# A two-layer graph attention network on one core: the carried row as column 0 of the one-hot matrix, nodes moved up by one

## The chip, the core and the metric

The kernel runs on one core of a Trainium2 chip. The core has five engines that run side by side, each with its own queue of instructions: TensorE (PE, matrix products into PSUM; PEld is its weight load), VectorE (DVE), ScalarE (ACT), GpSimd (POOL) and SyncE (SP, which here only issues DMAs). Data move between HBM and the on-chip memory through 16 DMA engines. The metric is the device time of one execution in microseconds (us); lower is better.

## The reference

There are 6,250 nodes with 256 features and 200,000 edges that are sorted by destination. After a layer norm and a ReLU come two graph attention layers (4 heads of 64, then 1 head of 256). In each, every edge has a logit, made of a value of its source, a value of its destination and a value of its 32 edge attributes; the logits go through a softmax over the edges of one destination; and the rows of the sources are summed with these weights at the destination. One loop edge per node, with the mean of the edge values, is added. Cut to what matters:

```python
te = relu(edge_attr @ We + be) * exp(x @ Wo + bo)[src][:, None]
s2, d2, ea2 = _add_self_loops(src, dst, te, n)
hx = (x @ Wg).reshape(n, h, f)
al = leaky_relu(a_s.hx[s2] + a_d.hx[d2] + a_e.(ea2 @ Wge), 0.2)
m = segment_max(al, d2)
al = exp(al - m[d2])
al = al / segment_sum(al, d2)[d2]
out = segment_sum(hx[s2] * al[:, :, None], d2) + b
```

## The kernel before

**Steps.** The sorted edges are cut into 66 steps of 24 x 128 = 3,072 edges (the last two are shorter). Both layers run through all steps, 132 in all. The edges of a step end at some 96 neighbouring nodes; `base` is the first of them. A node's place in a step is its number less `base`, and 128 places are provided for (partition = place).

**One step.** GpSimd gathers the source rows of the edges, 24 indirect DMAs of 128 rows each, into a tile G (three buffers), with a small memset between two gathers. TensorE makes the edge values from the attributes (`rphase1`, line 1014, and `rphase2`, line 1028) and spreads the destinations' values to the edges (`parts`, `adst`). VectorE adds the logits, runs maximum scans along the edges (`logits`, `links`, `maxima`; TensorE transposes in between, lines 1138 and 1155) and multiplies G by the weights (`scale`, line 1223). A one-hot matrix S (128 edges x 128 places, 24 of them; line 1058, VectorE) says which edge belongs to which place, and 24 accumulating products of S with G (`sums`, line 1234) sum the rows at the places. `evict` copies the sums from PSUM to U (line 1239, ScalarE). `finish` of the step before makes the output rows out of U.

**The carried row.** A node's edges can begin in one step and end in the next. So the sum of a step's last node is carried on: `carry` multiplies U by a one-hot column `lsel` (1 at the place of the last node) on TensorE (line 1245), which moves that row to partition 0, and copies it out of PSUM (line 1247, ScalarE). In the next step, after `scale`, `carried` adds this row, with a factor for the changed maximum, to edge 0 of partition 0 in G, ahead of `sums`.

**Order.** The order on each engine is written out by hand in `edges` (and `tight` and `last` for the last steps of a layer). In a full step k: GpSimd's gathers of step k+1; logits, transposes and maxima of k; edge values of k+1; scale, carried and sums of k; edge rows and one-hots of k+1; finish of k-1; evict and carry of k. Behind the carry on TensorE stand, in layer 0, the transposes of `turned` (line 1329), which write the same single PSUM buffer `fin`, and then the transpose of line 1138 of the next step.

**Loads and stores on SyncE.** `nodes` loads the node rows of a step, up to three steps ahead, into `tw` (five buffers): from table T, 268 columns in layer 0 (line 995), with x, 256 columns, beside it (line 997); 516 columns from the second table in layer 1. `load_ea` fetches edge attributes for two steps (one buffer, line 955), `load_lb` the places of the edges, which four groups of 32 partitions get as copies. `rows3` stores the rows of a finished step: 520 columns into the second table in layer 0 (line 1370), 256 into the output in layer 1 (line 1375; the last two steps by an indirect DMA). Neighbouring steps' rows overlap; the later store wins.

**Constants.** `kps` is a PSUM tile with the row 0..127 (`k_iota`), compared with each edge's place to give S, and its first 32 columns, compared for the smaller one-hot Q in `spread`. `qsel` and `lsel` are made in `indices`, which also counts whatever doesn't fit (more than 128 places and the like) into a flag; then a general path would compute everything again.

Of the kernel before, what the change touches and what calls it, by code (L numbers as in the profile page):

```python
# [22 lines left out]
F32 = mybir.dt.float32  # L23
# [8 lines left out]
P = 128  # L32
# [46 lines left out]
class Kernel:  # L79
# [31 lines left out]
    def consts(self, wp):  # L111
        nc, cp, a = self.nc, self.cp, self.a
        V = nc.vector
        self.ident = cp.tile([P, P], F32, name="ident")
        make_identity(nc, self.ident)
        self.wg, row, wpk = [], [], []
        self.ones = cp.tile([P, 1], F32, name="ones")
        nc.gpsimd.memset(self.ones, 1.0)
        self.bias, self.webd, self.be, wge = [], [], [], []
        for L in self.L:  # L120
            q = (nc.scalar, nc.sync)[L.l]
            wg = cp.tile([P, 2, L.MW], F32, name=f"wg{L.l}")
# [24 lines left out]
        self.kps = k = self.ps_k.tile([P, 512], F32, name="kps")  # L147
        V.tensor_copy(k[:, 0:P], self.iota_f)
        m32 = wp.tile([P, 1], F32, name="m32", bufs=1)
        self.quad = cp.tile([P, 4], F32, name="quad")  # L150
        nc.gpsimd.memset(self.quad, 0.0)
        for i in range(4):
            r = slice(32 * i, 32 * i + 32)
            nc.gpsimd.memset(m32[r, :], -32.0 * i)
            nc.gpsimd.memset(self.quad[r, i:i + 1], 1.0)
        V.tensor_add(k[:, P:P + 1], self.iota_p, m32)
        self.k_iota, self.k_part, self.k_w = k[:, 0:P], k[:, P:P + 1], k[:, 2 * P:2 * P + 4 * C + 4]
        self.wea = []
        for L in self.L:
            wea = cp.tile([P, PH], F32, name=f"wea{L.l}")  # L160
            nc.gpsimd.memset(wea, 0.0)
            self.wea.append((wea, cp.tile([P, L.H], F32, name=f"we1{L.l}")))

        def fold(L):

            H = L.H
            for k in range(2):
                for j, c0 in ((0, L.p), (1, L.ad)):
                    t = wp.tile([P, D], F32, name="wtmp", bufs=4)
                    V.tensor_mul(t, self.wg[L.l][:, k, 0:D], row[L.l][:, j, :])  # L170
                    yield
                    V.tensor_reduce(self.wg[L.l][:, k, c0:c0 + H], t.rearrange("p (h f) -> p h f", h=H),
                                    axis=AX.X, op=OP.add)
                    yield

        def fold_e(L):

            H = L.H
            wea, we1 = self.wea[L.l]
            t = wp.tile([P, D], F32, name="wtmp", bufs=4)  # L180
            V.tensor_mul(t, wge[L.l], row[L.l][:, 2, :])
# [12 lines left out]

        return fold(self.L[0]), later()
# [234 lines left out]
    def indices(self, wp):  # L430
# [26 lines left out]
        V.tensor_sub(qd, base.unsqueeze(1).to_broadcast([P, 4, NS]), qbase)  # L457
        yield
        self.qsel = cp.tile([P, NS, 4], F32, name="qsel")
        V.tensor_scalar(self.qsel.rearrange("p s k -> p k s"), qd, self.iota_p, None, op0=OP.add)  # L460
        yield

        bcf = wp.tile([NS, 4], F32, name="bcf", bufs=1)
# [31 lines left out]
        V.tensor_copy(self.base_i[:, 0, :], base[0:1, :])  # L495
        V.tensor_scalar(self.base_i[:, 1, :], base[0:1, :], float(N - P), None, op0=OP.min)
        yield
        ll = wp.tile([P, NS], F32, name="ll", bufs=1)
        V.tensor_sub(ll, last, base)
        self.lsel = cp.tile([P, NS], F32, name="lsel")  # L500
        V.tensor_scalar(self.lsel, ll, self.iota_p, None, op0=OP.is_equal)
        yield
        self.slink = cp.tile([1, NS], F32, name="slink")
        V.tensor_tensor(self.slink, sc0[0:1, 0, :], sc0[0:1, 2, :], op=OP.is_equal)
# [2 lines left out]

        chk = wp.tile([1, 9, NS + 1], F32, name="chk", bufs=1)
        V.memset(chk, 0.0)
        V.tensor_scalar(chk[:, 0, :NS], ll[0:1, :], float(P - 1), None, op0=OP.is_gt)  # L510
        V.tensor_sub(qd[0:1], qlast[0:1], qbase[0:1])
        V.tensor_scalar(chk[:, 5:9, :NS], qd[0:1], 31.0, None, op0=OP.is_gt)
        nb = wp.tile([1, NS + 1], F32, name="nb", bufs=1)
# [1 line left out]
        yield  # L515
        V.memset(nb[:, NS:], float(N))
        V.tensor_sub(nb[:, :NS], nb[:, 1:], nb[:, :NS])
        V.tensor_scalar(chk[:, 1, :NS], nb[:, :NS], float(P), None, op0=OP.is_gt)
# [92 lines left out]
    def edges(self, ctx):  # L611
# [11 lines left out]
        steps = self.steps  # L623
        self.state = {0: None, 1: None}
        self.early = 0
        self.nodes(steps[0])
        self.gather(steps[0], self.CX)
        if self.NS % 2:
# [15 lines left out]
        for k, st in enumerate(steps):  # L644
# [51 lines left out]
            if enter:  # L696
                pr = pv
            else:
                self.evict(st)
                self.carry(st)  # L700
                if pv:
                    self.rows1(pv)
                    late = pv
# [23 lines left out]
    def tight(self, st, pv, pr, nx):  # L727
# [36 lines left out]
            self.rows3(pv)  # L764
        drain(self.maxima(st))
        if final:
            self.carry(pv)
            drain(y)
            self.load_ea(st["k"] + 2)
        else:  # L770
# [1 line left out]
        self.rphase2(nx)  # L772
        self.adst(nx)
        if not final:
            self.carry(pv)
            if pr:
                self.rows1(pr)
                self.rows2(pr)
# [10 lines left out]
    def last(self, st, pv, nx):  # L789
# [20 lines left out]
        drain(self.maxima(st))  # L810
        if pv:
            self.evict(pv)
            self.carry(pv)
        drain(self.scale(st, 3))
        self.carried(st)
        self.sums(st)
# [172 lines left out]
    def nodes(self, st):  # L989
        nc, L, s = self.nc, st["L"], st["s"]  # L990
        r = self.row(0, s)
        tw = self.np_.tile([P, self.L[0].TW + D], F32, name="tw", bufs=5)
        st["tw"], st["xw"] = tw[:, :L.TW], tw[:, L.TW:L.TW + D]
        w = L.TW + L.l * D
        nc.sync.dma_start(tw[:, :w], self.T[L.l][ds(r, P), 0:w])
        if L.l == 0:
            nc.sync.dma_start(st["xw"], self.a["x"][ds(r, P), :])

    def halves(self, st):

# [30 lines left out]
    def spread(self, st):  # L1031
# [6 lines left out]
        if len(q) < 2 or q[0]["C"] != q[1]["C"]:  # L1038
# [3 lines left out]
        Q = self.wp.tile([P, 2, P], BF, name="Q")  # L1042
        V.tensor_tensor(lb[:, :, :n], lb[:, :, :n], self.k_part.unsqueeze(2).to_broadcast([P, i, n]), op=OP.is_equal)  # L1043
        V.tensor_tensor(Q[:, :i].rearrange("p i (k j) -> p (i k) j", j=32),
                        self.k_iota[:, 0:32].unsqueeze(1).to_broadcast([P, 4 * i, 32]),
                        self.qsel[:, s:s + i, :].rearrange("p i k -> p (i k)").unsqueeze(2)
                        .to_broadcast([P, 4 * i, 32]), op=OP.is_equal)
        for j, t in enumerate(q):
# [2 lines left out]
    def onehots(self, st, c0=0, c1=C):  # L1051
        nc, o = self.nc, st["o"]
        c1 = min(c1, st["C"])
        if "S" not in st:
            st["S"] = self.sp.tile([P, C, P], F32, name="S")
        if c0 < c1:
            w = [P, c1 - c0, P]
            nc.vector.tensor_tensor(st["S"][:, c0:c1, :], self.k_iota.unsqueeze(1).to_broadcast(w),  # L1058
# [138 lines left out]
    def carried(self, st):  # L1197


        if st["prev"] is not None:  # L1200
            L, V = st["L"], self.nc.vector
            H, pr = L.H, st["pr"]
            g, cv = st["G"][0:1, 0, :], st["prev"]["carry"]
            if H == 1:
                V.scalar_tensor_tensor(g[:, :D + 1], cv[0:1, :D + 1], pr[:, 0:1], g[:, :D + 1], op0=OP.mult, op1=OP.add)
            else:
# [29 lines left out]
    def evict(self, st):  # L1236
        L = st["L"]
        st["U"] = U = self.np_.tile([P, 272], F32, name="U", bufs=3)
        self.nc.scalar.activation(U[:, :L.W], st["u"][:, :L.W], AF.Copy)  # L1239

    def carry(self, st):
        nc, L, s, U = self.nc, st["L"], st["s"], st["U"]
        if s + 1 < self.NS:
            pr = self.ps_f.tile([P, 512], F32, name="fin")
            nc.tensor.matmul(pr[0:1, :L.W], self.lsel[:, s:s + 1], U[:, :L.W], start=True, stop=True)  # L1245
            st["carry"] = cv = self.wp.tile([1, 272], F32, name="carry")
            nc.scalar.activation(cv[:, :L.W], pr[0:1, :L.W], AF.Copy)

    def merge(self, st, wp, w):

# [114 lines left out]
    def rows3(self, st):  # L1365
        nc, L, s = self.nc, st["L"], st["s"]
        if L.l == 0:
            self.table_row(st)
            r = self.row(0, s)
            nc.sync.dma_start(self.T[1][ds(r, P), :], st["trow"])  # L1370
            return
        o, out = st["o"], self.a["out"]
        if s < self.direct:
            r = self.row(1, s)
            nc.sync.dma_start(out[ds(r, P), :], o)
        else:
            idx = self.np_.tile([P, 1], I32, name="oidx")
            nc.vector.tensor_add(idx, self.base_f[:, s:s + 1], self.iota_p)
            nc.gpsimd.indirect_dma_start(
                out=out[:, :], out_offset=bass.IndirectOffsetOnAxis(ap=idx[:, 0:1], axis=0), in_=o,  # L1380
                in_offset=None, bounds_check=self.N - 1, oob_is_err=False)
# [215 lines left out]
```

## Time and profile before

| | |
|---|---|
| device time, median of 3 runs | 4717.75 us (4715.25 to 4721.8) |
| the profiled execution, device time | 4718.23 us |
| its span on the core | 4716.0 us |
| TensorE busy (products) | 3214.2 us, 68% |
| VectorE busy | 2878.5 us, 61% |
| ScalarE busy | 574.2 us, 12% |
| GpSimd busy | 3701.8 us, 78% |
| gathers, GpSimd line 928 | 3102 issues, 0.959 us each |
| products u of `sums`, line 1234 | 6252 records, 393 ns each |
| carry: product, line 1245 | 260 records, 613 ns each |
| gather queue (q0) | 422.75 MB, 33.8% of the 16 DMA engines' span |
| SyncE's DMA queue (q1) | 158.16 MB, 10.1% |

The share of busy time says little by itself here: no engine is busy all the time, since a step is a chain over several engines. The prologue and the turn between the layers (about 2300 to 2530 us) apart, the span consists of equal steps, first of layer 0 and then of layer 1. The ends of TensorE's products in the trace are modelled: it records 24 products of `sums` in about 11 us, and the eviction that waits for the last of them begins some 19 us after the first.

```profile
PE   7777767777677776777655666666666666656666
DVE  7566767667676676766743555546455555645555
POOL 5688888888888888888648888888888888888884
DMA  6344444444444444444323444444444444444442
```

Each digit is the busy share, in tenths, in one of 40 equal slices of the span: one sees the two layers, and the turn in the middle.

### The profile page before, as it was taken

What the parts mean: (1) busy time and instruction counts of PE and PEld (TensorE: products, weight loads), DVE (VectorE), ACT (ScalarE), POOL (GpSimd) and SP (SyncE); (2) the same over time, 40 slices, a digit from 0 to 9 for tenths busy, and PEclk for the clock granted to TensorE, in tenths of its full rate; (3) what the DMA queues carried; (4) which work ended last, traced back from release to release, by engine and by line L of the source; (5) the groups of instructions that cost most, each with busy time, mean ns of one, the idle gap of its engine ahead of it and who ended that gap; (6) DMA issues with size and microseconds to landing.
All of it is one profiled execution on the core that took longest, in us unless ns stands there. A gap on an engine that the chain in (4) does not pass through costs nothing.

```text
span 4716.0 us, 38255 instructions
## 1 busy us (share of the span) xinstructions
PE 3214.2 (68%) x10176; PEld 1915.8 (41%) x10176; DVE 2878.5 (61%) x6552; ACT 574.2 (12%) x1282; POOL 3701.8 (78%) x6350
## 2 busy tenths in 40 slices
PE   7777767777677776777655666666666666656666
PEld 6444444444444443444422333434333343433334
DVE  7566767667676676766743555546455555645555
ACT  5111111111111111111100001000000100000010
POOL 5688888888888888888648888888888888888884
PEclk9677777767777777777866677777767776777778
DMA  6344444444444444444323444444444444444442
GB/s 216 111 129 126 136 122 129 134 122 135 127 134 127 124 136 123 132 131 124 107 84 104 128 118 126 125 112 127 120 127 118 126 126 111 127 118 128 118 124 63
DMA packets 236364, 584.09 MB, mean 124 GB/s; under 512 B 63097, under 2 KB 91007, under 8 KB 236073
## 3 DMA queue, kind: packets, MB, share of 16 engines
q0 software_dynamic: 150144, 422.75, 33.8%
q1 hardware_dynamic: 85579, 158.16, 10.1%
q8 instruction: 82, 1.34, 0.1%
q14 instruction: 143, 1.17, 0.1%
q10 hardware_dynamic: 416, 0.67, 0.1%
HBM read 547.11 MB, written 34.33 MB: 123 GB/s over the span
## 4 chain that ended last, share of the span: by engine, by line
DVE 40%; another core or an unknown queue 33%; PE 16%; issue 6%; ACT 4%; POOL 0%; DMA 0%; SPq 0%; DVEq 0%; ACTq 0%; POOLq 0%
DVE G L1223 16%; DVE S L1058 8%; PE y L1014 8%; PE fin L1245 3%; DVE rt L1101 2%; ACT R L1019 1%; ACT U L1239 1%; DVE ade L1104 1%; PE fin L1329 1%; PE u L1234 1%; PE lf L1138 1%; PE zad L1028 1%; DVE mt L1172 1%; DVE m L1175 1%
## 5 line engine op out<-in xcount | busy, mean ns | idle before, releaser
L928 POOL DMA_INDIRECT G<-T,src x3102 | 2974.0, 959 | 938.3 <-issue 498.2
L1234 PE MATMUL u<-G,S 128*128 128x270 f32 (+1 forms) x6252 | 1469.7, 393 | 110.3 <-issue 58.0
L1234 PEld LDWEIGHTS u<-G,S 128*128 128x128 f32 x6252 | 1186.9, 192 | 394.5 <-issue 87.1
L1245 PE MATMUL fin<-U,lsel 128*1 128x270 f32 (+1 forms) x260 | 132.8, 613 | 1143.3 <-ACT U L1239 1136.6
L1223 DVE TENSOR_TENSOR G<-G,kps 128x6144 f32<-128x6144 f32 (+2 forms) x140 | 853.3, 6100 | 0.0
L1014 PE MATMUL y<-ea,webd 64*128 64x384 f32 (+1 forms) x1056 | 754.6, 866 | 89.2 <-issue 65.5
L932 POOL MEMSET gap<- 128x128 f32 x3102 | 684.6, 221 | 4.3 <-remote 1.3
L1148 DVE TENSOR_TENSOR_SCAN cl<-fl,cl,lf 4x129 f32<-4x129 f32 (+1 forms) x130 | 61.2, 471 | 1016.6 <-PE zad L1073 994.3
L1245 PEld LDWEIGHTS fin<-U,lsel 128*1 128x1 f32 x260 | 11.1, 81 | 1202.6 <-ACT U L1239 1201.5
L1028 PE MATMUL zad<-R,wea 128*64 128x384 f32 (+1 forms) x1056 | 474.0, 816 | 0.3 <-DVE aq L1080 0.3
L1014 PEld LDWEIGHTS y<-ea,webd 64*128 64x128 f32 x1056 | 303.3, 317 | 360.3 <-issue 330.0
L1058 DVE TENSOR_TENSOR S<-kps,loc 128x3072 f32<-128x3072 f32 x132 | 436.2, 3305 | 0.0
L1019 ACT ACTIVATE R<-y,webd 128x768 f32<-128x768 f32 x260 | 232.9, 896 | 794.6 <-PE y L1014 348.3
L1028 PEld LDWEIGHTS zad<-R,wea 128*64 128x64 f32 x1056 | 160.4, 207 | 314.9 <-issue 248.5
L1239 ACT ACTIVATE U<-u 128x270 f32<-128x270 f32 (+1 forms) x132 | 51.8, 393 | 1627.1 <-remote 1585.4
L1101 DVE STREAM_TRANSPOSE rt<-zad 128x768 f32<-128x768 f32 (+1 forms) x130 | 125.0, 961 | 27.8 <-remote 15.7
L424 PE MATMUL fin<-wg,h1T 128*128 128x260 f32 x264 | 135.7, 669 | 3.2 <-ACT h1T L1331 3.2
L1043 DVE TENSOR_TENSOR lb<-lb,kps 128x1536 bf16<-128x1536 bf16 (+1 forms) x68 | 113.0, 1662 | 0.0
L424 PE MATMUL ps<-wg,hT 128*128 128x266 f32 x292 | 89.8, 435 | 25.4 <-ACT hT L311 13.9
L424 PEld LDWEIGHTS fin<-wg,h1T 128*128 128x128 f32 x264 | 76.0, 317 | 53.7 <-issue 36.3
L1272 ACT ACTIVATE mw<-mw,mg 128x2 f32<-128x2 f32 x66 | 19.7, 298 | 557.3 <-DVE mw L1264 249.1
L1138 PE MATMUL lf<-ident,fb 128*36 128x128 f32 (+1 forms) x132 | 54.9, 416 | 42.8 <-DVE al L1119 28.2
(193 smaller groups left out, 2269.0 us busy)
## 6 DMA issues: line engine op xcount, KB each, us to landing
G<-T,src POOLq DMA_INDIRECT x3102
ea<-in_ea_dram SPq DMA_DIRECT2D x64, 768.0 KB
lb<-locrow SPq DMA_DIRECT2D x64, 384.0 KB
T<-t1row SPq DMA_DIRECT2D x66, 260.0 KB
tw<-T SPq DMA_DIRECT2D x66, 258.0 KB
tw<-T SPq DMA_DIRECT2D x66, 134.0 KB
tw<-in_x_dram SPq DMA_DIRECT2D x66, 128.0 KB
out_dram<-fb SPq DMA_DIRECT2D x64, 128.0 KB
```

Of the source, the lines that this page charges most:

```text
L424: self.nc.tensor.matmul(ps[:, :L.MW], hT[:, k, :], self.wg[L.l][:, k, :], start=(k == 0), stop=(k == 1))
L928: nc.gpsimd.indirect_dma_start(out=G[:, c, 0:L.TW], out_offset=None, in_=self.rows[L.l][0:n * (1 + L.l), :], in_offset=bass.IndirectOffset ...
L932: nc.gpsimd.memset(self.gap, 0.0)
L1014: nc.tensor.matmul(y[:, o], self.webd[l][r, :], ea[r, w], start=True, stop=True)
L1019: nc.scalar.activation(R[:, i, :32 * c].rearrange("p (b n) -> p b n", b=2), y.rearrange("p (b n) -> p b n", b=2)[:, :, :16 * c], AF.Relu, ...
L1028: nc.tensor.matmul(st["zad"][i * PH:(i + 1) * PH, o], self.wea[l][0], R[:, i, w], start=True, stop=False)
L1043: V.tensor_tensor(lb[:, :, :n], lb[:, :, :n], self.k_part.unsqueeze(2).to_broadcast([P, i, n]), op=OP.is_equal)
L1058: nc.vector.tensor_tensor(st["S"][:, c0:c1, :], self.k_iota.unsqueeze(1).to_broadcast(w), self.loc[:, o + c0:o + c1].unsqueeze(2).to_broad ...
L1101: V.transpose(rv[:, :32 * c].rearrange("p (b n) -> p b n", b=2), z.rearrange("p (b n) -> p b n", b=2)[:, :, :16 * c])
L1223: nc.vector.tensor_tensor(v, v, pw[:, c0:c1, :].unsqueeze(3) .to_broadcast([P, c1 - c0, H, L.F]), op=OP.mult)
L1234: nc.tensor.matmul(st["u"][:, :L.W], S[:, i, :], G[:, i, 0:L.W], start=(j == 0), stop=(j == c - 1))
L1245: nc.tensor.matmul(pr[0:1, :L.W], self.lsel[:, s:s + 1], U[:, :L.W], start=True, stop=True)
```

## The change

Place 0 is given to the carried row. The row in `k_iota` now begins with -1, so an edge of place j finds its 1 in column j+1 of S: all nodes move up by one partition. Column 0 of `k_iota` is overwritten in each step with the place of the step's last node (`lastloc`), so that column 0 of S sums the last node's edges once more, and the sums leave its row in partition 0 of U. `carried` reads it there; `carry`, its product and its copy are gone, as is `lsel`. Everything by node follows: loads and stores leave out partition 0 and take 127 rows; five `tw` tiles are kept by name, with partition 0 cleared once; `qsel` and the output indices use a column that begins with -1; Q compares with a separate row 0..31; the checks for the flag allow 127 places.

```diff
-        V.tensor_copy(k[:, 0:P], self.iota_f)
+        V.tensor_scalar(k[:, 0:P], self.iota_f, -1.0, None, op0=OP.add)
+        V.tensor_copy(k[:, P + 2:P + 34], self.iota_f[:, 0:32])
+        self.iota_m = cp.tile([P, 1], F32, name="iota_m")
+        nc.gpsimd.iota(self.iota_m, pattern=[[0, 1]], base=-1, channel_multiplier=1,
+                       allow_small_or_imprecise_dtypes=True)
...
-        ll = wp.tile([P, NS], F32, name="ll", bufs=1)
+        self.lastloc = ll = cp.tile([P, NS], F32, name="lastloc")
         V.tensor_sub(ll, last, base)
-        self.lsel = cp.tile([P, NS], F32, name="lsel")
-        V.tensor_scalar(self.lsel, ll, self.iota_p, None, op0=OP.is_equal)
...
+        self.tws = [self.np_.tile([P, self.L[0].TW + D], F32, name=f"tw{i}", bufs=1) for i in range(5)]
+        for t in self.tws:
+            nc.vector.memset(t[0:1, :], 0.0)
...
                 self.evict(st)
-                self.carry(st)
...
     def nodes(self, st):
-        tw = self.np_.tile([P, self.L[0].TW + D], F32, name="tw", bufs=5)
+        tw = self.tws[st["k"] % 5]
...
-        nc.sync.dma_start(tw[:, :w], self.T[L.l][ds(r, P), 0:w])
+        nc.sync.dma_start(tw[1:P, :w], self.T[L.l][ds(r, P - 1), 0:w])
         if L.l == 0:
-            nc.sync.dma_start(st["xw"], self.a["x"][ds(r, P), :])
+            nc.sync.dma_start(st["xw"][1:P, :], self.a["x"][ds(r, P - 1), :])
...
     def onehots(self, st, c0=0, c1=C):
         if "S" not in st:
             st["S"] = self.sp.tile([P, C, P], F32, name="S")
+            nc.vector.tensor_copy(self.k_iota[:, 0:1], self.lastloc[:, st["s"]:st["s"] + 1])
...
     def carried(self, st):
-            g, cv = st["G"][0:1, 0, :], st["prev"]["carry"]
+            g, cv = st["G"][0:1, 0, :], st["prev"]["U"]
...
-    def carry(self, st):
-        nc, L, s, U = self.nc, st["L"], st["s"], st["U"]
-        if s + 1 < self.NS:
-            pr = self.ps_f.tile([P, 512], F32, name="fin")
-            nc.tensor.matmul(pr[0:1, :L.W], self.lsel[:, s:s + 1], U[:, :L.W], start=True, stop=True)
-            st["carry"] = cv = self.wp.tile([1, 272], F32, name="carry")
-            nc.scalar.activation(cv[:, :L.W], pr[0:1, :L.W], AF.Copy)
...
     def rows3(self, st):
-            nc.sync.dma_start(self.T[1][ds(r, P), :], st["trow"])
+            nc.sync.dma_start(self.T[1][ds(r, P - 1), :], st["trow"][1:P, :])
...
-            nc.sync.dma_start(out[ds(r, P), :], o)
+            nc.sync.dma_start(out[ds(r, P - 1), :], o[1:P, :])
         else:
-            nc.vector.tensor_add(idx, self.base_f[:, s:s + 1], self.iota_p)
+            nc.vector.tensor_add(idx, self.base_f[:, s:s + 1], self.iota_m)
+            nc.vector.memset(idx[0:1, :], 1 << 20)
```

More of the change, by code (lines that the diff above doesn't have):

```diff
@@ L156, in consts @@
         V.tensor_add(k[:, P:P + 1], self.iota_p, m32)
-        self.k_iota, self.k_part, self.k_w = k[:, 0:P], k[:, P:P + 1], k[:, 2 * P:2 * P + 4 * C + 4]
+        self.k_iota, self.k_part, self.k_32 = k[:, 0:P], k[:, P:P + 1], k[:, P + 2:P + 34]
+        self.k_w = k[:, 2 * P:2 * P + 4 * C + 4]
         self.wea = []
@@ L459, in indices @@
         self.qsel = cp.tile([P, NS, 4], F32, name="qsel")
-        V.tensor_scalar(self.qsel.rearrange("p s k -> p k s"), qd, self.iota_p, None, op0=OP.add)
+        V.tensor_scalar(self.qsel.rearrange("p s k -> p k s"), qd, self.iota_m, None, op0=OP.add)
         yield
@@ L509, in indices @@
         V.memset(chk, 0.0)
-        V.tensor_scalar(chk[:, 0, :NS], ll[0:1, :], float(P - 1), None, op0=OP.is_gt)
+        V.tensor_scalar(chk[:, 0, :NS], ll[0:1, :], float(P - 2), None, op0=OP.is_gt)
         V.tensor_sub(qd[0:1], qlast[0:1], qbase[0:1])
@@ L517, in indices @@
         V.tensor_sub(nb[:, :NS], nb[:, 1:], nb[:, :NS])
-        V.tensor_scalar(chk[:, 1, :NS], nb[:, :NS], float(P), None, op0=OP.is_gt)
+        V.tensor_scalar(chk[:, 1, :NS], nb[:, :NS], float(P - 1), None, op0=OP.is_gt)
         V.tensor_scalar(chk[:, 2, :NS], nb[:, :NS], 0.0, None, op0=OP.is_lt)
@@ L766, in tight @@
         if final:
-            self.carry(pv)
             drain(y)
@@ L774, in tight @@
         if not final:
-            self.carry(pv)
             if pr:
@@ L812, in last @@
             self.evict(pv)
-            self.carry(pv)
         drain(self.scale(st, 3))
@@ L1044, in spread @@
         V.tensor_tensor(Q[:, :i].rearrange("p i (k j) -> p (i k) j", j=32),
-                        self.k_iota[:, 0:32].unsqueeze(1).to_broadcast([P, 4 * i, 32]),
+                        self.k_32.unsqueeze(1).to_broadcast([P, 4 * i, 32]),
                         self.qsel[:, s:s + i, :].rearrange("p i k -> p (i k)").unsqueeze(2)
```

## The prediction

> **What bounds the kernel now.** I read first where the last chain of waits spends the span, then one step of it in each layer, then GpSimd's own waits, then the DMA issues and, packet by packet, the trace's DMA records. The chain by engine and line, and the groups of the product that goes:
>
> ```profile
> DVE 40%; another core or an unknown queue 33%; PE 16%; issue 6%; ACT 4%; POOL 0%; DMA 0%; SPq 0%; DVEq 0%; ACTq 0%; POOLq 0%
> L1245 PE MATMUL fin<-U,lsel 128*1 128x270 f32 (+1 forms) x260 | 132.8, 613 | 1143.3 <-ACT U L1239 1136.6
> L1239 ACT ACTIVATE U<-u 128x270 f32<-128x270 f32 (+1 forms) x132 | 51.8, 393 | 1627.1 <-remote 1585.4
> ```
>
> The 33% "unknown queue" stands ahead of the eviction U (line 1239): it is the true length of the 24 products of sums(), whose ends the profile only models. TensorE seems idle for 1143 us ahead of line 1245, but most of that is its own products draining. What can go is what lies behind the drain. The chain of waits in a step of layer 0, then of layer 1 (start, us, what):
>
> ```profile
> 1015.11 0.41 ACT U L1239
> 1015.56 1.07 PE fin L1245 x2
> 1016.66 0.40 ACT carry L1247
> 1017.10 0.69 PE fin L1329 x2
> 1017.79 0.21 PE lf L1138
> ...
> 3519.72 0.40 ACT U L1239
> 3520.16 1.03 PE fin L1245 x2
> 3521.19 0.35 PE lf L1138
> ```
>
> Both layers run one closed loop: sums on TensorE (19.0 us from first product to eviction in layer 0, 21.1 in layer 1), carry, the transposes of line 1138, scans and maxima on VectorE, scale (line 1223, 6.5 us), sums again. A step is 34.6 us in layer 0 (59 steps between GpSimd's waits at 220 and 2261) and 34.4 in layer 1 (58 steps, 2557 to 4553). The carry is on this loop each time.
>
> **The gain.** Without the carry, TensorE goes on when its products end, just before U starts. Layer 0: line 1329 starts at 1015.1 instead of 1017.10, 2.0 us (it waited for the carry's copy to free the one fin buffer). Layer 1: line 1138 starts at 3519.7 instead of 3521.19, 1.45 us with the overlap of the eviction. The 130 products (260 records) and 130 copies vanish; U is still made, but is first needed by carried(), 14 us later, behind scale. Next limits: VectorE's wait ahead of the scan of line 1148 is 12 to 14 us in layer 1, so all of the 1.45 counts; in layer 0 it is 2.9 us in the median of 58 steps and under 2.0 in every third or so, and the smaller of 2.0 and the wait is 1.65 on average. GpSimd's 24 gathers take 24 x (0.95 + 0.22 + 0.17) = 32.2 us a step, and it waits about 2.2 us more at each first gather, until the sums free a buffer:
>
> ```profile
> 1015.35 0.95 POOL L928 DMA_INDIRECT G<-T,src  x1 [2.36 <-remote]
> 3519.95 0.95 POOL L928 DMA_INDIRECT G<-T,src  x1 [2.23 <-remote]
> ```
>
> So steps of 32.95 us in both layers are free of GpSimd's limit. Taken alone: 60 x 1.65 + 62 x 1.45 = 99 + 90 = 189 us.
>
> **The small additions.** 132 copies of one column (like the 128x1 cast of line 1068, 0.13 us: 17 us in all) stand on VectorE ahead of S (line 1058), which is wanted a step later: nothing in layer 1, whose cover is the 12 us wait; if that cover were gone, 9 us per layer. S itself keeps its 3.3 us, sums its 24 products. Five memsets, two iotas and two cleared indices come once: under 2 us. SyncE issues the same DMAs in the same order.
>
> **The 127 rows.** Every load of tw (line 995) and x (997) and every store of T1 (1370) and out (1375) loses a row. The issues:
>
> ```profile
> ea<-in_ea_dram SPq DMA_DIRECT2D x64, 768.0 KB
> lb<-locrow SPq DMA_DIRECT2D x64, 384.0 KB
> T<-t1row SPq DMA_DIRECT2D x66, 260.0 KB
> tw<-T SPq DMA_DIRECT2D x66, 258.0 KB
> tw<-T SPq DMA_DIRECT2D x66, 134.0 KB
> tw<-in_x_dram SPq DMA_DIRECT2D x66, 128.0 KB
> out_dram<-fb SPq DMA_DIRECT2D x64, 128.0 KB
> ```
>
> How many DMA engines a transfer uses can be read from the DMA records, by how many of its packets run at once. The ea load (256 rows over 128 partitions) runs some 12 to 14 at once and is done in 3 us. The lb load has half the bytes, but a leading dimension of 4: at most 4 streams, 6 to 7 us. The prologue's 66-row drow runs 11.1 at once from 34.7 to 37.2 us, and its 106-row zero store runs as exactly two streams of rows 45 ns apart. The count is a divisor of the rows: 128 gives 16, 66 gives 11, 106 gives 2. For 127, a prime, it is 1. And it is the same engines each time: the 66-row r4, issued behind drow, starts at 37.3, as drow ends, while src, issued behind r4, starts at 32.6 on the engines left free. So all 127 rows of each of these transfers should queue on one engine, always the same, which has its sixteenth of the gathers too.
>
> The Trainium skill, "DMA: Bandwidth & Descriptors", section "Why a DMA increments its semaphore by 16 and not by 1", says so outright: the number of engines is the largest divisor up to 16 of the slowest dimension, 127 partitions get 1, and SyncE's DMAs take the lowest-numbered engines. The trace agrees for 106, 66 and 4; none of its transfers has 127 rows. By that rule the sum is the one below; without it, the 189 us would be gained whole.
>
> What that engine does in a step of layer 0, row by row from the records (duration; starts are 3 ns closer): 127 x (48 ns for tw's 1072 B + 46 for x's 1024 B + 85 for T1's 2080 B) = 22.7 us, or 21.6 by starts; its 8 rows of ea at 0.12 = 1.0; 16 rows of lb (it is one of the 4) = 1.9; small ones 0.3. Together 24.8 to 25.9, where it has 3.5 now. To this come 24 x 2 packets of the gathers. One lasts 0.165 us when the engine has just read the same gather, 0.255 on average: 7.9 or 12.2 us a step. What it costs beside a full queue the lb load shows: 96 of its 128 rows (24 per stream, 2.8 us of their own) take 4.26 us on average, in which 6.4 gather packets pass, so 0.22 each. tw's and x's rows are a third as long as lb's and hide less of a gather's first read, so I take 0.23: 11.1 us. Sum for the engine: 25.4 + 11.1 + 0.2 of completion writes = 36.7 us, from 32.7 (7.9) to 38.3 (12.2). That is over the 32.95 of the shortened loop and over the 34.6 of now: layer 0 becomes bound by one DMA engine, with ea's load (line 955), due a step after its issue, or tw as what the loop waits for. The queue must first fill (an ea load is issued some 26 us ahead of its use and needs 3 now; the queue grows by 2 to 4 us a step), so of 66 steps 58 pay: 58 x (36.7 - 34.6) = +122 us; at the ends 32.95, so -99, and 38.3, so +215.
>
> Layer 1 has no x load and a smaller store: 127 x (85 + 46) = 16.6, with ea, lb and small 3.1, and 48 gather packets at 0.18 (same reading of lb there; 0.16 to 0.25) 8.7: 28.4 us, at most 31.7, under 32.95. It keeps its gain of 90 us.
>
> The turn between layers: the gathers of layer 1 wait for the last T1 store, now 127 x 0.085 = 10.8 us on one engine instead of about 1, partly behind the one before: +12. The four short steps at the layers' ends save their carry: -6. First loads of tw in each layer lie under the 32 us of the first gathers.
>
> **Sum**, against the profiled execution's 4718.2 us (span 4716.0; the median is 4717.75, the same for this purpose): +122 - 90 + 12 - 6 = +38, so 4756 us. With the queue's price at its ends: 4718 - 99 - 90 + 6 = 4535 and 4718 + 215 - 90 + 6 = 4849.
>
> **Rivals.**
> One: faster, since the engine keeps up (or the rows are spread after all). For it: a gather packet behind another takes 0.165, not 0.23, and an engine with more queued could read ahead; all other engines are some 45% busy. Then both layers run near 32.95: 4535 us; at 0.19 a packet the layer-0 step is about 34.8 and the time about 4650. It decides from a layer-0 step of 36.05 downward, where 58 x 1.45 = 84 equals what the rest gains. Against it: the lb load beside the gathers.
> Two: worse, because the queue costs more than its throughput: SyncE issues in order, an ea load stands behind a T1 store of 10.8 us, loads come late in layer 1 too, and its 90 us are lost: 4756 + 90 = 4846; with gathers at 0.255 as well, 4940. For it: one ea buffer. Against it: in layer 1 the engine has 1 to 4 us a step to spare and tw is loaded over 50 us ahead.
> Three: the carry was not the loop's limit, the wait only moves to the scan. Then nothing is gained, and with the queue 4718 + 122 + 12 = 4852. Against it: VectorE's 12 to 14 us of waiting in layer 1.
>
> **Chances.** Forecast (a layer-0 step of 35.4 to 37.9 us, 4680 to 4825): 0.55, some of it below the 36.05 of no change. Rival one: 0.25. Rivals two and three: 0.14 and 0.06. The range leaves out the lower half of rival one and the upper end of two: 4580 to 4880; the likeliest case's own is 4680 to 4825. No change means within 0.2%, about what a measurement of this kernel can tell, 4708 to 4727. Faster 0.25 + 0.13 = 0.38, same 0.06, slower 0.56.
>
> **What would show it.** Lines 1245 and 1247 are gone; in layer 1 line 1138 follows the sums by under 0.1 us and a step is 32.9 us; GpSimd's wait at the first gather there falls to about 0.7. In layer 0 a step is near 36.7, the new wait is of TensorE's line 1014 on ea or of VectorE on tw, and SyncE waits for earlier DMAs. In the DMA records rows of 1072, 1024 and 2080 B run one at a time, 127 in a line. Wrong: these rows run 16 at once, or layer-0 steps under 34 us (rival one), or layer-1 steps over 34 us (two or three).

## The result, and the profile after

| | before | after |
|---|---|---|
| device time, median | 4716.69 us (4715.25 to 4721.8, 6 runs) | 4749.73 us (4737.5 to 4759.65, 6 runs) |
| ratio | | 1.0068 (95% interval 1.005 to 1.0086) |
| span of the profiled execution | 4716.0 us | 4743.5 us |

The changed kernel is 33 us slower; 4756 was predicted. In some of the experiments below the kernel before itself took 4377 to 4383 us instead of 4717, with no difference in the kernel, so every ratio here is to the runs of the kernel before in the same set, and each set is named by that time: "set 4717" or "set 4380".

The page of the changed kernel, first the chain that ended last by engine, then three groups (busy us and mean ns of one, then idle time ahead of them and its main releaser). Line numbers have moved by two to five: 928 is now 930, 1148 is 1151, 1239 is 1242.

```profile
DVE 38%; POOL 20%; another core or an unknown queue 19%; issue 9%; PE 6%; DMA 3%; SPq 3%; ACT 1%; DVEq 0%; POOLq 0%; ACTq 0%
L930 POOL DMA_INDIRECT G<-T,src x3102 | 2966.9, 956 | 965.9 <-issue 498.4
L1151 DVE TENSOR_TENSOR_SCAN cl<-fl,cl,lf 4x129 f32<-4x129 f32 (+1 forms) x130 | 61.2, 471 | 1173.9 <-remote 1094.8
L1242 ACT ACTIVATE U<-u 128x270 f32<-128x270 f32 (+1 forms) x132 | 51.9, 393 | 2002.7 <-remote 1677.5
```

The carry's groups are gone, and TensorE's part of the chain fell from 16% to 6% (the carry's product alone was 3%), but what they took has turned into waiting: ScalarE waits 2002.7 us ahead of the evictions of U (1627.1 before), VectorE 1173.9 ahead of the first scan (1016.6 before), and GpSimd 965.9 ahead of its gathers (938.3 before). The last two groups and one scan of layer 1 in the kernel before:

```profile
L928 POOL DMA_INDIRECT G<-T,src x3102 | 2974.0, 959 | 938.3 <-issue 498.2
L1148 DVE TENSOR_TENSOR_SCAN cl<-fl,cl,lf 4x129 f32<-4x129 f32 (+1 forms) x130 | 61.2, 471 | 1016.6 <-PE zad L1073 994.3
3521.58 0.47 DVE L1148 TENSOR_TENSOR_SCAN cl<-fl,cl,lf 1x129 f32<-1x129 f32 x1 [13.80 <-PE zad L1073]
```

One step of layer 1 of the changed kernel (start us, us, engine and line; in brackets the idle time before it and what ended that):

```profile
3538.46 0.95 POOL L930 DMA_INDIRECT G<-T,src  x1 [0.17 <-issue]
3541.81 0.39 ACT L1242 ACTIVATE U<-u 128x261 f32<-128x261 f32 x1 [18.83 <-remote]
3541.84 0.47 DVE L1151 TENSOR_TENSOR_SCAN cl<-fl,cl,lf 1x129 f32<-1x129 f32 x1 [15.33 <-remote]
3542.05 0.95 POOL L930 DMA_INDIRECT G<-T,src  x1 [2.41 <-remote]
```

The scan now starts 0.03 us behind the eviction; before it was 1.86 us behind it (3521.58 against 3519.72). So the carry is off its place, as meant. But the eviction comes that much later, and GpSimd's first gather still waits, 2.41 us where it was 2.23. A step of layer 1 takes 34.38 us in the median, and took 34.40.

Where the 27.5 us of span went is seen by cutting it at the starts of VectorE's full-size scales (line 1223, now 1226; the small scales of a layer's last steps fall into the turn and the rest), times in us:

| | to the first scale | layer 0, first to last scale | turn, to the next scale | layer 1, to the last scale | rest |
|---|---|---|---|---|---|
| before | 166.9 | 2163.3 | 132.8 | 2186.4 | 66.6 |
| after | 175.1 | 2161.7 | 151.4 | 2182.3 | 73.0 |

Both layers take what they took (-1.6 and -4.1 us); the prologue, the turn and the end are 8.2, 18.6 and 6.4 us longer. The two layers' differences are small beside the 22 us between the fastest and the slowest run of the changed kernel (in after_again, below, they are -6.7 and +0.7). The prologue, the turn and the end are the places where SyncE's loads and stores are not covered by other work. SyncE's queue of the changed kernel, at the first node loads and in the middle of layer 0:

```profile
143.04 0.32 SPq L997 DMA_DIRECT2D tw<-T  x1
143.57 1.53 SPq L999 DMA_DIRECT2D tw<-in_x_dram  x1
145.88 6.70 SPq L997 DMA_DIRECT2D tw<-T  x1
152.76 8.49 SPq L999 DMA_DIRECT2D tw<-in_x_dram  x1
...
1106.40 8.56 SPq L997 DMA_DIRECT2D tw<-T  x1
1115.15 10.90 SPq L999 DMA_DIRECT2D tw<-in_x_dram  x1
1126.11 6.94 SPq L957 DMA_DIRECT2D lb<-locrow  x1
```

and of the kernel before at the same place:

```profile
145.19 0.33 SPq L995 DMA_DIRECT2D tw<-T  x1
145.71 0.33 SPq L997 DMA_DIRECT2D tw<-in_x_dram  x1
```

An issue of 127 rows goes through at once twice, and from the third on SyncE is held 7 to 17 us by each, and then by the lb load behind it. From 400 to 2200 us SyncE spends 1496 us in issues, and 76 before. The DMA records suggest why. From 1000 to 1150 us the rows of 1072, 1024 and 2080 B start 45, 47 and 82 ns apart in the median and never more than two overlap, the next starting a few ns ahead of the end of one; before, up to 16, 18 and 19 overlap. The trace does not name the engines, but this is what one DMA engine that takes all these rows, one behind the other, would show, with SyncE let go when enough of them are through.

### The profile page after: what moved, and what is told of

The parts are those of the page before. It is cut to its first block, busy times and chain, and to the rows that moved or that the text cites. A ratio compares the mean times of both kernels' runs of the same rounds, so it can differ in the third digit from the quotient of the medians.

```text
span 4743.5 us, 37627 instructions
## 1 busy us (share of the span) xinstructions
PE 3038.2 (64%) x9916; PEld 1893.0 (40%) x9916; DVE 2892.5 (61%) x6691; ACT 508.3 (11%) x1152; POOL 3694.7 (78%) x6351
## 4 chain that ended last, share of the span: by engine, by line
DVE 38%; POOL 20%; another core or an unknown queue 19%; issue 9%; PE 6%; DMA 3%; SPq 3%; ACT 1%; DVEq 0%; POOLq 0%; ACTq 0%
POOL G L930 16%; DVE G L1226 11%; DVE S L1061 6%; POOL gap L934 4%; PE y L1016 2%; PE u L1237 2%; DVE lb L1045 2%; DVE rt L1104 2%; DMA gi<-in_dnx_dram 1%; SPq L999 1%; DMA T<-t1row 1%; PE ps L429 1%; SPq L997 1%; DVE al L1124 1%
## 5 line engine op out<-in xcount | busy, mean ns | idle before, releaser
L930 POOL DMA_INDIRECT G<-T,src x3102 | 2966.9, 956 | 965.9 <-issue 498.4
L1237 PE MATMUL u<-G,S 128*128 128x270 f32 (+1 forms) x6252 | 1517.1, 402 | 201.8 <-issue 112.3
L1237 PEld LDWEIGHTS u<-G,S 128*128 128x128 f32 x6252 | 1217.0, 197 | 505.1 <-issue 136.5
L1151 DVE TENSOR_TENSOR_SCAN cl<-fl,cl,lf 4x129 f32<-4x129 f32 (+1 forms) x130 | 61.2, 471 | 1173.9 <-remote 1094.8
L1016 PE MATMUL y<-ea,webd 64*128 64x384 f32 (+1 forms) x1056 | 667.0, 774 | 41.3 <-ACT R L1021 20.3
L1158 PE MATMUL lf<-ident,cl 36*128 36x36 f32 (+1 forms) x132 | 39.8, 302 | 895.5 <-DVE cl L1153 890.7
L1158 PEld LDWEIGHTS lf<-ident,cl 36*128 36x128 f32 (+1 forms) x132 | 24.7, 187 | 984.9 <-DVE cl L1153 971.9
L1016 PEld LDWEIGHTS y<-ea,webd 64*128 64x128 f32 x1056 | 270.6, 283 | 243.0 <-issue 183.1
L1242 ACT ACTIVATE U<-u 128x270 f32<-128x270 f32 (+1 forms) x132 | 51.9, 393 | 2002.7 <-remote 1677.5
L1141 PE MATMUL lf<-ident,fb 128*36 128x128 f32 (+1 forms) x132 | 41.3, 313 | 267.7 <-DVE fb L1133 160.8
L1076 PE MATMUL zad<-a,Q 128*128 128x12 bf16 (+1 forms) x132 | 23.9, 181 | 230.7 <-DVE a L1074 181.4
L1141 PEld LDWEIGHTS lf<-ident,fb 128*36 128x36 f32 (+1 forms) x132 | 14.4, 109 | 293.7 <-DVE fb L1133 171.5
```

Of the source, the lines that this page charges most:

```text
L930: nc.gpsimd.indirect_dma_start(out=G[:, c, 0:L.TW], out_offset=None, in_=self.rows[L.l][0:n * (1 + L.l), :], in_offset=bass.IndirectOffset ...
L1016: nc.tensor.matmul(y[:, o], self.webd[l][r, :], ea[r, w], start=True, stop=True)
L1158: nc.tensor.transpose(pc, cl[:n, 0:P], self.ident[0:n, 0:n])
L1237: nc.tensor.matmul(st["u"][:, :L.W], S[:, i, :], G[:, i, 0:L.W], start=(j == 0), stop=(j == c - 1))
```

## The experiments

**Is the carry on the loop that limits?** Three kernels: the carry left out of the kernel before, put back into the changed one, and doubled.

before_nocarry (set 4717):

```diff
-                self.carry(st)
...
-            g, cv = st["G"][0:1, 0, :], st["prev"]["carry"]
+            g, cv = st["G"][0:1, 0, :], st["prev"]["U"]
```

> The kernel before, without the carry's product and copy (lines 1245 and 1247); the step reads row 0 of the last sums where it read the carried row, so the result differs. If the carry lies on the loop that limits the steps, as predicted, the steps fall to 32.95 us and the time to about 4525 us. If GpSimd's batch of 24 gathers (24 x 1.34 = 32.1 us) and the 2.2 us until the sums are released set the step, whatever the carry does, the steps stay at 34.6 and 34.4 us, the time at 4717 us within 10, and the eviction of the sums only moves to about 23.4 us (layer 0) and 24.5 us (layer 1) after the first product, from 19.0 and 21.1.

Measured: 4742.42 us, 1.0047 (1.003 to 1.0064). No gain; a small loss. The eviction moved as the second theory said, to 23.3 us (layer 0) and 24.4 us (layer 1) behind the first product, from 19.0 and 21.1 (medians); the time missed that theory too, which allowed 10 us. Two kinds of steps are seen in its layer 1 (eviction, and GpSimd's gathers around it):

```profile
2653.28 0.39 ACT L1235 ACTIVATE U<-u 128x261 f32<-128x261 f32 x1 [19.10 <-remote]
2653.52 0.95 POOL L924 DMA_INDIRECT G<-T,src  x1 [2.31 <-remote]
...
2684.59 0.95 POOL L924 DMA_INDIRECT G<-T,src  x1 [0.17 <-issue]
2685.50 0.39 ACT L1235 ACTIVATE U<-u 128x261 f32<-128x261 f32 x1 [16.90 <-remote]
2685.93 0.95 POOL L924 DMA_INDIRECT G<-T,src  x1 [0.17 <-issue]
...
2727.65 0.39 ACT L1235 ACTIVATE U<-u 128x261 f32<-128x261 f32 x1 [0.77 <-PE u L1230]
2727.89 1.05 POOL L924 DMA_INDIRECT G<-T,src  x1 [8.50 <-PE u L1230]
```

The usual step ends like 2653: the batch of gathers ends, the eviction follows, the next batch starts. At 2685 the eviction came 0.9 us after the start of the batch's last gather, GpSimd went on without a break, and the next eviction was 42 us away, with an 8.50 us wait. In this profile 20 of 62 steps of layer 1 are over 34.8 us (one before, four in the changed kernel), and layer 1 takes 2236.0 us where it took 2186.4. The loss lies there; this execution, of 4761 us, was the slowest of the four.

after_carry (set 4717):

```diff
+            nc.tensor.matmul(pr[0:1, :L.W], self.ident[:, 0:1], U[:, :L.W], start=True, stop=True)
+            nc.scalar.activation(cv[:, :L.W], pr[0:1, :L.W], AF.Copy)
```

> The changed kernel with a carry product and copy put back (a one-hot column picks row 0 of U). If the carry is on the limiting loop, it adds 2.0 us to each step of layer 0 and 1.45 to each of layer 1: 4750 + 210 = 4960 us. If GpSimd's batch sets the step: 4750 us within 10, with the eviction again 19 to 21 us behind the first product.

Measured: 4740.98 us, 1.0054 (1.0037 to 1.0071), the same as the changed kernel within the intervals, not the 4960 of a carry on the limiting loop. The evictions are back at 18.9 and 21.2 us.

before_twocarry (set 4380):

```diff
+            nc.tensor.matmul(pr[0:1, :L.W], self.ones[0:1, 0:1], cv[:, :L.W], start=True, stop=True)
+            nc.scalar.activation(cv[:, :L.W], pr[0:1, :L.W], AF.Copy)
```

> The kernel before with a second product and copy behind each carry (the row is multiplied by one and copied again), 1.5 us more between the sums and the scans. If the carry lies on the loop that limits the steps: +1.5 us a step, 125 x 1.5 = +190 us. If it only fills a wait for GpSimd's batch: no change within 10 us, with the eviction 1.5 us less behind the first product (about 17.4 and 19.6 us).

Measured: 4385.59 us against 4377.49, 1.0019 (1.0007 to 1.003): 8 us, not 190. This speaks for set 4380 alone, where the eviction does not stand where it did in set 4717. The evictions did not come at 17.4 and 19.6 us, but 11.3 and 10.9 us behind the first product: in this set the sums are released as their records end. One step, with the sums, and gathers before and behind the eviction:

```profile
1115.22 11.21 PE L1234 MATMUL u<-G,S 128*128 128x270 f32 x48 [1.40 <-DVE G L1213]
1125.86 0.95 POOL L928 DMA_INDIRECT G<-T,src  x1 [0.17 <-issue]
1126.47 0.40 ACT L1239 ACTIVATE U<-u 128x270 f32<-128x270 f32 x1 [1.91 <-PE u L1234]
1127.19 0.95 POOL L928 DMA_INDIRECT G<-T,src  x1 [0.17 <-issue]
```

and the chain on its page:

```profile
POOL 80%; issue 12%; PE 4%; DVE 3%; DMA 1%; ACT 0%; POOLq 0%; SPq 0%; DVEq 0%; ACTq 0%
```

GpSimd issues gathers with no break and is four fifths of the chain (most of the rest is its issue time). Neither carry is on it.

**What do the 127 rows cost?**

after_split (set 4717):

```diff
-        nc.sync.dma_start(tw[1:P, :w], self.T[L.l][ds(r, P - 1), 0:w])
+        for p0, n in ((0, 112), (112, 15)):
+            nc.sync.dma_start(tw[1 + p0:1 + p0 + n, :w], self.T[L.l][ds(r + p0, n), 0:w])
```

and likewise for x and both stores.

> The changed kernel with each 127-row transfer issued as one of 112 rows and one of 15. If one busy DMA engine held layer 0 up and the carry was a real gain, as predicted: about 4535 us, steps of 32.95 us. If GpSimd's batch sets the steps and the 127-row transfers cost only the prologue, the turn between the layers and the end: steps of 34.4 to 34.6 us as now, and 4750 less some 27 to 33 us, so 4717 to 4723 us, equal to the kernel before.

Measured: 4726.68 us, 1.0024 (1.0014 to 1.0034): two thirds of the loss are gone, and nothing of a gain of 180 us appears; the second case's 4717 to 4723 us was missed by 4. First scale at 168.5, turn 133.9, end 66.6: the prologue, the turn and the end are those of the kernel before again. In the window of 1000 to 1150 us up to 17 to 20 of the rows overlap. SyncE spends 145 us in issues from 400 to 2200 us, not 1496. The remaining 10 us lie in the layers (2169.1 and 2190.2), where more steps take over 35 us (14 in layer 0, 5 in layer 1; before 5 and 1); why they do was not tried.

after_again (set 4717) is the changed kernel, unchanged:

> The changed kernel once more, on another chip. Theory G: GpSimd's batch sets the step in both kernels, so the change costs only its 127-row transfers. Where the kernel before takes 4717 us: a ratio of 1.005 to 1.009. Where the kernel before takes 4383 us (the sums are released 11 us behind the first product there, and GpSimd issues gathers without a break, 32.1 us a step): 4383 + 30 = about 4413 us if one DMA engine still keeps up with 127-row transfers within 32.1 us a step, and 58 x 2 to 58 x 4.6 us more, 4530 to 4680 us, if that engine needs 34 to 36.7 us a step in layer 0, as predicted.

Measured: 4754.59 us, 1.0088 (1.0071 to 1.0104).

after_third, the same kernel again, fell into set 4380:

> The changed kernel a third time. Where the kernel before takes 4717 us: 4740 to 4760 us again. Where it takes 4383 us: 4413 us if only the ends pay for the 127-row transfers, 4530 to 4680 us if one DMA engine needs 34 to 36.7 us a step in layer 0.

Measured: 4554.42 us against 4377.49, 1.0404 (1.0374 to 1.0435), inside the range for one DMA engine that sets layer 0. Cut as above, with before_twocarry as the nearest profile of the kernel before in this set:

| | to the first scale | layer 0 | turn | layer 1 | rest |
|---|---|---|---|---|---|
| before_twocarry | 139.0 | 2002.2 | 134.8 | 2036.9 | 70.7 |
| after_third | 149.6 | 2160.2 | 150.4 | 2026.1 | 64.0 |

Layer 0 loses 158 us, layer 1 nothing. In layer 0 four steps together take 139.3 us (1095.5 to 1234.7 us), 34.8 each. SyncE's queue in after_third:

```profile
1096.05 10.92 SPq L999 DMA_DIRECT2D tw<-in_x_dram  x1
1107.02 7.70 SPq L957 DMA_DIRECT2D lb<-locrow  x1
...
1119.64 16.16 SPq L997 DMA_DIRECT2D tw<-T  x1
```

and the chain of waits in it, from 1080 us (start us, us, what):

```profile
1076.61 15.27 DMA fl<-flags
...
1095.62 6.40 DVE G L1226
...
1103.04 11.21 PE u L1237 x48
...
1116.62 13.67 DMA gi<-in_dnx_dram
```

SyncE is held in issues for 1675 of 1800 us (400 to 2200), and the small loads behind the held issues (the flags, the indices) come late: once in four steps, the chain goes through them. Layer 0 takes the same 2160 us here as in set 4717. If this queue sets every step, it needs some 34.8 us a step (48 steps from 468 us on); in set 4717 that nearly fits under steps that take 34.6 us anyway, and in set 4380, where the same 48 steps of before_twocarry take 32.4 each, it shows. The split rows alone were not run in this set; the pause kernels below, which have them, come nearest.

**Is GpSimd's batch the loop?**

before_nogap (set 4717):

```diff
-            if st["k"]:
-                nc.gpsimd.memset(self.gap, 0.0)
```

> The kernel before without the memset behind each gather (line 932), which makes GpSimd's batch 24 x 1.12 = 26.9 us. If the chain of sums, carry, scans and scale is the limit, the steps stay at 34.4 us and the time at 4717 us within 20. If GpSimd's batch sets the step, steps fall to about 29 us (26.9 + 2.2, or where the chain of TensorE and VectorE ends first) and the time to some 4050 to 4300 us. A time above 4717 us would mean that gathers issued closer together delay something else.

Measured: 4847.71 us, 1.0278 (1.0258 to 1.0299), the third of the cases named: a gather now follows the last by 1.25 us (30.1 us a batch), but the evictions come 21.2 us (layer 0) and 21.7 us behind the first product, and GpSimd waits longer:

```profile
1156.24 0.95 POOL L928 DMA_INDIRECT G<-T,src  x1 [0.30 <-issue]
1161.73 0.95 POOL L928 DMA_INDIRECT G<-T,src  x1 [4.54 <-remote]
...
1190.56 0.95 POOL L928 DMA_INDIRECT G<-T,src  x1 [0.30 <-issue]
1198.70 0.95 POOL L928 DMA_INDIRECT G<-T,src  x1 [7.19 <-PE u L1232]
```

Steps go to 36.1 us (layer 0) and 34.95 us (layer 1). The products of the same step, with the eviction:

```profile
1177.09 8.93 PE L1232 MATMUL u<-G,S 128*128 128x270 f32 x38 [1.36 <-DVE crow L1209]
1187.66 0.39 PE L1232 MATMUL u<-G,S 128*128 128x270 f32 x1 [1.65 <-issue]
1189.76 0.39 PE L1232 MATMUL u<-G,S 128*128 128x270 f32 x1 [1.72 <-issue]
1192.57 0.61 PE L1232 MATMUL u<-G,S 128*128 128x270 f32 x1 [2.42 <-issue]
1194.66 3.77 PE L1232 MATMUL u<-G,S 128*128 128x270 f32 x7 [1.48 <-issue]
1198.46 0.40 ACT L1237 ACTIVATE U<-u 128x270 f32<-128x270 f32 x1 [9.66 <-PE u L1232]
```

Of the 48 records 38 run in 8.93 us. The next three come one by one, each behind 1.65 to 2.42 us of idle time, and the last seven run together from 4.1 us after the start of the batch's last gather (1190.56). The eviction follows the last record at once, here and in the median of the steps (0.04 us). So in this kernel the trace shows the last products themselves late, and not only the release behind them. With the 128-column memset the records end 11 us behind the first and the eviction comes 8 to 14 us later; there the trace does not tell the two apart. In set 4717 the release seems to depend on the gathers beside the sums, and denser gathers went with a later one.

before_longgap (set 4380): the memset's tile is 200 columns wide, not 128.

> The kernel before with the memset behind each gather widened from 128 to 200 columns, by the row of 32 columns (0.14 us) and that of 128 (0.22 us) about 0.06 us each, 24 x 0.06 = 1.4 us a batch. Theory G (a step is GpSimd's batch and a fixed 2.2 us until the sums are released): steps +1.4 us, +175 us in all. Theory T (a fixed throughput of about 34.4 us a step, of which the 2.2 us wait is only the rest): the wait shrinks to about 0.8 us, the steps stay. Where the kernel before takes 4383 us, GpSimd issues without a break and both say +175 us.

Measured: 4542.05 us, 1.0376 (1.0346 to 1.0406), 165 us of the 175. In this set GpSimd's batch alone sets the step. Which of G and T holds in set 4717 was not decided.

Then a pause in the middle of a batch, to see whether the release follows it:

```diff
-                nc.gpsimd.memset(self.gap, 0.0)
+                nc.gpsimd.memset(self.gap[:, :32], 0.0)
+                for _ in range(6 if j == 17 else 0):
+                    nc.gpsimd.memset(self.gap, 0.0)
```

This is split_pause_short. split_pause keeps the 128 columns; before_pause_short is the kernel before with the pause at j == 21.

> after_split with five more memsets (5 x 0.39 us) on GpSimd behind the 18th of the 24 gathers, a pause of some 2 us at a time when all 48 records of the sums have started. Theory P: the sums are released only when the gathers pause, now at the end of each batch. Then the eviction follows the pause, about 15 to 17 us behind the first product instead of 23.3 and 24.5, GpSimd no longer waits at the first gather of a batch, and the step is its 32.1 + 2.0 + 0.2 = 34.3 us: time within 20 us of 4727. Theory D: the sums need their 23 to 24 us by themselves beside gathers. Then the eviction stays there and GpSimd waits about 0.5 us at the end; the time is the same, only the eviction tells.

> after_split with the memset behind each gather cut from 128 to 32 columns, and a pause of six memsets of 128 columns behind the 18th gather. Theory P: the eviction follows the pause, the step is GpSimd's: 24 gathers at about 1.22 us plus 2.3, some 31.6 us, and the time falls by 125 x 2.8 = 350 us to about 4380. Theory D: the release stays 23 to 25 us behind the first product, GpSimd waits some 3 us at the end of the batch, steps stay at 34 to 36 us and the time between 4700 and 4850 us, as it did without the memsets (4848).

> The kernel before with the same short memsets and the pause behind the 22nd gather (its sums start some 4 us later in the batch). Theory P: steps near 31.6 us as well, if TensorE and VectorE with the carry fit into them, and a time near 4370; if the carry then lies on the chain that limits, the step is longer than in split_pause_short by up to its 1.5 to 2.0 us. Theory D: as for split_pause_short, 4700 to 4850 us.

All three fell into set 4380, where the sums are released after 11 us anyway, so they decide nothing between P and D: 4540.37 us, 1.0359 (1.0329 to 1.0389); 4333.68 us, 0.9888 (0.9849 to 0.9926); 4328.47 us, 0.9876 (0.9847 to 0.9905). They show another thing: with the rows split, the kernel without the carry and the kernel with it take the same time (layer 0 1978.9 and 1979.4 us, layer 1 2006.5 and 2009.4). Without the held queue the change neither costs nor gains where GpSimd sets the step.

short_again is split_pause_short in set 4717:

> split_pause_short once more, on another chip. Where the kernel before takes 4717 us. Theory P (release needs a pause of the gathers): eviction follows the pause behind the 18th gather, steps near 31.5 us, time near 4350 us. Theory D (the sums need 22 to 25 us beside gathers whatever the pause): steps of 34 to 36 us, 4700 to 4850 us. Where the kernel before takes 4383 us: 4334 us again, and nothing is decided.

Measured: 4779.43 us, 1.0136 (1.0115 to 1.0156), with steps of 34.97 and 34.4 us, inside D's ranges. In layer 0, and in 41 of 64 steps of layer 1, the eviction did not come in the pause: the gathers on its two sides start 2.83 us apart (median), and the eviction follows some 10 us later, at the end of the batch, 21.7 us (layer 0) and 24.5 us (layer 1) behind the first product. That does not refute P. The pause is shorter than the 3.2 to 3.5 us that lie between the last gather's start and the eviction at the end of a batch, and it seems to come too early: in layer 0 it lies some 8.6 to 11.4 us behind the first product, but the last record of the sums ends only 20.6 us behind it (medians): here too the last products come late. In the other 23 steps of layer 1 the pause grew to between 3.5 and 6.0 us, and in nine of them the eviction came in it, as here:

```profile
3007.17 0.95 POOL L930 DMA_INDIRECT G<-T,src  x1 [0.17 <-issue]
3008.32 0.47 POOL L936 MEMSET gap<- 128x128 f32 x2
3009.78 0.20 POOL L936 MEMSET gap<- 128x128 f32 x1 [0.99 <-issue]
3010.48 0.20 POOL L936 MEMSET gap<- 128x128 f32 x1 [0.50 <-POOL gap L936]
3011.89 0.47 POOL L936 MEMSET gap<- 128x128 f32 x2 [1.20 <-POOL gap L936]
3012.18 0.39 ACT L1245 ACTIVATE U<-u 128x261 f32<-128x261 f32 x1 [16.85 <-remote]
3012.51 0.95 POOL L930 DMA_INDIRECT G<-T,src  x1 [0.16 <-issue]
```

Six memsets that took 1.5 us in split_pause_short, and in most steps of this run, took 4.0 here, and the first gather behind them does not wait for the sums, yet starts right behind their release. Neither P nor D foretold that, and what stretched the memsets stays open. A version that beats both kernels in both sets was not found: the short memsets gain 1.1 to 1.2% in set 4380, and lost 1.4% in set 4717.

## Why the prediction was right, and where it was wrong

The time was met (4756, measured 4750), but by luck: two errors cancel. The sum was +122 for layer 0 and -90 for layer 1; the profile shows -1.6 and -4.1, so a loss of 122 and a gain of 90 both failed to come. The rest was to be +12 - 6 = +6 us and was +33.2.

- **The loop of sums, carry, scans and scale: wrong.** The step that failed is "So steps of 32.95 us in both layers are free of GpSimd's limit". The same paragraph had GpSimd's 32.2 us and its 2.2 us of waiting, which add up to the step, and took the wait for something that shrinks with the carry. It did not: 2.23 us before, 2.41 after, and the steps of layer 1 stayed at 34.38 us, over the 34 that the prediction itself named as a sign of being wrong. In set 4717, in every kernel with the 128-column memset, the eviction starts 3.2 to 3.5 us (medians) behind the start of the batch's last gather, whether the products began 10.9 us (changed kernel, layer 0) or 15.4 us into the batch (before). In that set leaving the carry out and putting it back moved the eviction by 3.3 to 4.4 us, and neither gained anything; in set 4380 doubling it cost 8 us.
- **"The true length of the 24 products": wrong.** The 19.0 and 21.1 us were read as TensorE's work. The changed kernel took 23.3 and 24.5 us for as many products, and in set 4380 they took 11.3 and 10.9, so the time is not the products' own.
- **VectorE's wait of 12 to 14 us as evidence against rival three: wrong.** It proves that VectorE waits, not for whom. It grew to 15.3 us.
- **127 rows on one engine, always the same: right as far as the records show**, to within 4 ns in the rows' spacing (45, 47 and 82 ns, with 45, 43 and 82 worked out from the durations less 3 ns). SyncE's waiting behind it was expected, but as waits for earlier DMAs; it is the issue itself that is held.
- **A layer-0 step of 36.7 us: the size was off.** Set 4380 shows 34.8 where this queue sets the step. If the engine is never idle there, the 25.4 us of its own rows and 0.2 of completions leave 9.2 us for 48 gather packets, 0.19 us each, where 0.23 was taken. At 34.8 the prediction's own rule gives 58 x 0.2 = 12 us against the 34.6 of before, and set 4717 shows still less: -1.6 us, not +122.
- **Layer 1 under its limit: right** (2182.3 against 2186.4 us; 2026.1 against 2036.9).
- **The turn, +12: the rows as its cause right, the size 18.6 and, in set 4380, 15.6 us.** With the rows split it is 1.1 us.
- **The first loads of tw, free: wrong**, 8.2 us in the profile and 10.6 in set 4380; split, 1.6. In the first steps SyncE is held while the loads behind are wanted soon.
- **The short steps, -6: not seen.** The end was 6.4 us longer in this profile, 1.2 in after_again.
- **The small additions, expected to cost nothing: nothing is seen of them.** The column's copy takes 0.15 us; no run tried it alone.

Of the cases, rival three had the mechanism of the layers (0.06 was too little), without its 122 us; what is left of the loss is the forecast's own mechanism at the ends. In set 4380, where the layers are not otherwise held at 34.4 us, the same mechanism costs 4%.

## What to carry to other kernels

When two engines' loops add up to the same step, as GpSimd's 32.1 + 2.3 us did here, a piece taken out of one of them may gain nothing until the other is shown to be free: look for the engine whose own work plus one wait is the period, and ask whether that wait really shrinks. Before cutting a 128-row transfer by a row, look at how many of its packets run at once; 112 + 15 rows cost one more issue each and gave two thirds of the lost time back here. And a gain that is read from the "unknown queue" ahead of a wait should be tested by moving the start of the work: if the end stays, as it stayed here 3.2 to 3.5 us behind the last gather, the work alone was not what took the time.

## What the runs showed of the hardware that was not expected

- A transfer that runs on one DMA engine holds its issuer: two issues of 127 rows go through in 0.3 and 1.5 us, the third and fourth take 6.7 and 8.5 us, and beside gathers up to 17 us (19.6 in after_third). Everything behind them in SyncE's queue waits.
- One kernel, two times: 4717 and 4380 us, in two sets on one and the same chip. In set 4717 the sums are released 19 to 25 us behind the first product and mostly when the gathers have stopped (the step at 2685 us of before_nocarry is an exception); in set 4380 after 11 us. The traces differ in two more ways: the first holds 22,573 records of semaphore updates (before), the second 70,598 to 75,334 (the three pause kernels); and the granted clock of the kernel before is 0.73 in the first and 0.76 in the second, 4% apart, which is too little by itself for 11 us to become 19. That many completions are neither recorded nor passed on in time is one reading; the records of before_nogap, where the last products themselves come late, speak for another, that TensorE is held between products. What holds it was not tried and stays open.
- In set 4717 a step of some 34.4 to 35 us came out of three different loops (with the carry, without it, and with 30.2 us of gathers and a pause of 2.8 us in most steps), which looks like a fixed throughput, but denser gathers without a pause gave 35 to 36 us. This too is open.
